# Two rows of turns of their own: for the first three groups, and for what is left once the last group has begun

## The chip, the cores and the metric

The kernel runs on one core of a Trainium2 chip. Its engines work side by side, each through its own queue: TensorE (PE, with its weight loads as PEld), VectorE (DVE), ScalarE (ACT), GpSimd (POOL) and SyncE (SP), which here only issues transfers. The metric is the device time of one execution in microseconds (us), the median over runs.

## What is computed

Four graph layers are applied one after the other to 64 graphs of 256 nodes with 256 features; each layer gets the features x and the graph's adjacency matrix, and its result is added to x and normalised:

```python
x = layernorm(x + L0(x, adj))   # q, k, v projections, 4 heads, masked softmax, Wo, layernorm
x = layernorm(x + L1(x, adj))   # layernorm, 8 heads with q = k = v, masked softmax,
                                # layernorm, gelu(y @ W1 + b1) @ W2 + b2 (256 -> 1024 -> 256)
x = layernorm(x + L2(x, adj))   # Wh = x @ W; e = leaky_relu(s1[i] + s2[j]), masked softmax, e @ Wh
x = layernorm(x + L3(x, adj))   # e = leaky_relu((x * a0) @ x.T), softmax where adj == 1, e @ x
```

All is float32. The graphs don't depend on each other; within a graph the layers do.

## The kernel before

**Groups.** The 64 graphs are worked in 32 groups of two (`G = 2`). A graph of 256 nodes is two blocks of 128 rows, so a group's activations are tiles of 128 partitions x 4 blocks x 256 features. A group is a Python generator, `group(g)`: it records the instructions of a small step and yields. A call of `next` on it is a *turn*. Its steps in order:

- one turn to load x and adj of the group (SP, L439 and L441; for groups 0 and 1 the loads are already recorded ahead of the weights W1 and W2),
- one turn in which ACT turns adj into bfloat16 (`adjb`, L875, and a check, L876),
- one turn for the transposes of `adjb` by DMA (`adjT`, L883, four instructions on SP), then the mask on DVE (L886), which multiplies adjT by adjb,
- layer 0: transposes of x by PE (L519 `pm<-ident,x`) and their copy by ACT (`xT`, L572), projections with Wq and Wk (ACT writes `qT`, `kT`, L699) and Wv, then attention,
- layer 1: the same attention with q = k = v and eight heads, W1 with a gelu (`hT`, L774) and W2 (`project`, y at L687),
- layer 2 (`wx` projection, `ex`, the matrix `qT` at L829 and L831, the product `v,qT`) and layer 3 (`ps<-z,xT`, exponentials L857 and L858, DVE L859 and L861, the product `xn,qT`).

Every matmul is recorded at L516 and every PE transpose at L519, whatever the step, so the tiles tell them apart.

**Attention.** A chunk makes scores on PE (`ps`), ACT takes the exponential (`e`, L593), DVE multiplies by the mask: in layer 0 one instruction per tile (L595), in layer 1 one per 128 x 256 piece with a running sum (L601), 8 per chunk, 4 chunks per group. The products `e,v` or `e,z` of a chunk follow on PE after the scores of the next chunk. What comes after the products of a graph (`behind`) is spread over later turns. In layer 0 it is: the sums' reciprocals (`zs`, L629) go to DRAM (`lines`, L714) and come back spread over the partitions (`rr`, L716), DVE multiplies (`oT`, L718), PE multiplies with Wo (`pm<-L_gnn_WoT,oT`), DVE adds the bias (y, L725), then two normalisations (L532, L533 and L729 to L736 on DVE, L535 and L539 on POOL) lead to `z` and `xb`, which layer 1 starts from.

**Order.** PE's order is the order in which the turns are recorded: `in_order` ties each matmul to the one before. The order on the other engines is chosen when the program is built, by priorities that follow the recording and by what is ready in the builder's own reckoning; once built, each engine works through its queue from front to back. So the row of turns sets what stands behind what on every engine.

In steady state five to six groups of different ages are under way. One period of turns is `ORDER`, 45 digits; a digit is an age, and the group that gets the turn is `period - age`. Every group gets 45 turns in all: 1 in the period in which it begins, then 9, 13, 13, 6 and 3. The loop runs over 32 + 5 periods and leaves out groups that don't exist. In the first and the last periods the same row is thus played with holes: at the start a group's turns follow each other with few of other groups between them, and at the end likewise.

**Buffers.** x and adj have two buffers each (`io`), `adjb` and `adjT` one each, so a group's `adjb` waits for the mask of the group before it. Most activations have three (`AT_ONCE`), PSUM four tiles `pm` and two `ps`.

`prepare` is a further generator that makes constants (bias products, `bop`, `wx` columns, bounds); it goes forward one step with each turn of group 0 after the first five (`PREPARE`).

Of the kernel before, what the change touches and what calls it, by code (L numbers as in the profile page):

```python
# [32 lines left out]
END = "end"  # L33
AT_ONCE = 3


ORDER = "011225334342343542234235432323132121321132121"
PREPARE = 5


# [355 lines left out]
def usual_input(ctx: ExitStack, tc: tile.TileContext, a: dict, out: bass.AP, flag: bass.AP):  # L396
# [574 lines left out]

    groups = [group(g) for g in range(B // G)]
    preparing = prepare()
    own = 0
    for period in range(len(groups) + int(max(ORDER))):
        for age in ORDER:
            g = period - int(age)
            if 0 <= g < len(groups):
                next(groups[g], END)
            if g == 0:  # L980
                own += 1
                if own > PREPARE:
                    next(preparing, END)
    assert all(next(g, END) == END for g in groups)


# [18 lines left out]
@with_exitstack  # L1005
def four_layers(ctx: ExitStack, tc: tile.TileContext, a: dict, out: bass.AP):
    nc = tc.nc
    keep = ctx.enter_context(tc.tile_pool(name="keep", bufs=1))
    flag = keep.tile([1, 1], I32, name="flag")
    usual_input(tc, a, out, flag)  # L1010
    unusual = nc.values_load(flag)
    with tc.If(unusual > 0):
        any_input(tc, a, out)
# [25 lines left out]
```

## Time and profile before

| | before |
|---|---|
| device time, median of 3 | 2674.66 us (2673.68 to 2675.3) |
| span of the profiled execution | 2673.3 us, granted TensorE clock 0.989 |
| PE busy | 2589.8 us (97%) |
| DVE busy | 1968.5 us (74%) |
| ACT busy | 1291.3 us (48%) |
| POOL busy | 587.3 us (22%) |
| the chain that ended last | PE 70%, DVE 17%, POOL 9% |

A row of the profile names the engine, the line, the operation, the tile it writes and the tiles it reads, and how many instructions it stands for; in brackets is the idle time of the engine just before it and what ended it. Idle time of an engine that others don't wait for costs nothing. The granted clock is the share of its full speed at which TensorE was let run. What is read from these views, stretch by stretch, is in the prediction.

### The profile page before, as it was taken

How to read it: one execution, taken by the hardware profiler on the slowest of the kernel's cores; microseconds unless marked ns; L12 is line 12 of the kernel's file. 1: busy time of each engine (PE TensorE's matmuls, PEld its weight loads, DVE VectorE, ACT ScalarE, POOL GpSimd, SP SyncE). 2: the span in 40 equal slices, each digit the busy share in tenths (PEclk: the TensorE clock that was granted, in tenths of full speed). 3: DMA queues.
4: the chain of work that ended last, by engine and by line, in shares of the span. 5: the costliest groups of instructions: out<-in, count | busy, mean ns of one | idle time of the engine just before them, and what ended most of it. 6: DMA issues, size and time to landing. Idle time of an engine off the chain costs nothing.

```text
span 2673.3 us, 44868 instructions
## 1 busy us (share of the span) xinstructions
PE 2589.8 (97%) x16648; PEld 1764.3 (66%) x16648; DVE 1968.5 (74%) x6189; ACT 1291.3 (48%) x1995; POOL 587.3 (22%) x1139
## 2 busy tenths in 40 slices
PE   5899999999999999999999999999999999999996
PEld 2466676676676676676676676676676676676665
DVE  4657777777777777777777777777777777777764
ACT  3445444555444555444455444455445455445442
POOL 1212222222222222222222222222222222222221
PEclk8899999999999999999999999999999999999998
DMA  5000110010110010110010110010110010000000
GB/s 154 25 9 22 35 37 25 29 36 21 36 36 25 29 37 21 36 37 25 29 36 21 36 36 25 29 35 22 36 36 25 29 32 25 29 29 17 17 9 17
DMA packets 113728, 83.20 MB, mean 31 GB/s; under 512 B 44256, under 2 KB 113120, under 8 KB 113504
## 3 DMA queue, kind: packets, MB, share of 16 engines
q1 hardware_dynamic: 112416, 79.74, 9.9%
q8 instruction: 134, 2.20, 0.3%
q14 instruction: 90, 0.74, 0.1%
q10 hardware_dynamic: 1088, 0.53, 0.1%
HBM read 54.80 MB, written 17.04 MB: 27 GB/s over the span
## 4 chain that ended last, share of the span: by engine, by line
PE 70%; DVE 17%; POOL 9%; issue 2%; DMA 1%; SPq 1%; ACT 0%; DVEq 0%; POOLq 0%; ACTq 0%
PE pm L516 54%; PE ps L516 10%; PE pm L519 7%; POOL rstd L539 6%; DVE st L532 3%; DVE y L802 2%; DVE y L730 2%; DVE xn L547 2%; POOL ve L535 2%; DVE z L547 2%; DVE mv L533 1%; DVE y L729 1%; DVE xb L736 1%; DVE e L601 1%; DVE r L801 1%
## 5 line engine op out<-in xcount | busy, mean ns | idle before, releaser
L601 DVE SCALAR_TENSOR_TENSOR e<-e,mask 128x256 f32<-128x256 f32 x1024 | 430.3, 486 | 131.6 <-ACT e L593 131.6
L593 ACT ACTIVATE e<-ps 128x1024 f32<-128x1024 f32 x384 | 371.9, 1019 | 195.1 <-PE ps L516 178.4
L516 PE MATMUL pm<-L_gnn_W,hT 128*128 128x256 f32 x2048 | 462.7, 379 | 0.0
L516 PE MATMUL pm<-xT,L_gnn_W 128*128 128x512 f32 x1024 | 456.2, 594 | 0.0
L516 PEld LDWEIGHTS pm<-L_gnn_W,hT 128*128 128x128 f32 x2048 | 384.6, 190 | 48.8 <-issue 0.3
L774 ACT ACTIVATE hT<-pm,b 128x512 f32<-128x512 f32 x256 | 176.9, 691 | 417.7 <-PE pm L516 417.6
L516 PEld LDWEIGHTS pm<-xT,L_gnn_W 128*128 128x128 f32 x1024 | 192.6, 191 | 204.5 <-issue 199.7
L532 DVE BATCH_NORM_STATS2 st<-y 128x6 f32<-128x256 f32 x768 | 301.4, 408 | 6.7
L539 POOL TENSOR_TENSOR rstd<-ve,mhalf 128x2 f32<-128x2 f32 (+1 forms) x384 | 298.1, 776 | 26.6
L547 DVE TENSOR_SCALAR xn<-y,mv,rstd 128x256 f32<-128x256 f32 x384 | 141.6, 410 | 180.1 <-POOL rstd L539 180.1
L535 POOL TENSOR_SCALAR ve<-mv 128x2 f32<-128x2 f32 x384 | 98.5, 257 | 757.7 <-DVE mv L533 757.2
L760 POOL TENSOR_TENSOR both<-y,xb 128x512 f32<-128x512 f32 x64 | 81.3, 1271 | 761.7 <-DVE y L759 761.7
L595 DVE TENSOR_TENSOR e<-e,mask 128x1024 f32<-128x1024 f32 x128 | 150.9, 1221 | 17.1 <-ACT e L593 17.1
L574 ACT ACTIVATE xT<-pm,beta,gamma 128x512 f32<-128x512 f32 x128 | 92.4, 770 | 126.1 <-PE pm L519 125.9
L516 PE MATMUL ps<-xT 32*128 32x256 f32 x2048 | 148.5, 402 | 0.3 <-ACT e L593 0.2
L516 PE MATMUL pm<-e,z 128*32 128x256 f32 x2048 | 141.3, 385 | 1.7 <-DVE e L601 1.4
L516 PEld LDWEIGHTS ps<-xT 32*128 32x128 f32 x2048 | 93.4, 185 | 72.8 <-issue 68.3
L516 PE MATMUL pm<-L_gnn_WoT,oT 128*128 128x256 f32 x512 | 120.4, 389 | 14.7 <-DVE oT L718 12.5
L516 PE MATMUL pm<-e,v 128*32 128x256 f32 x2048 | 125.2, 384 | 6.0 <-DVE e L595 6.0
L516 PE MATMUL ps<-qT,kT 64*128 64x256 f32 x1024 | 127.9, 389 | 0.3 <-ACT e L593 0.3
L516 PE MATMUL pm<-xT,L_gnn_WqT 128*128 128x512 f32 x256 | 121.5, 618 | 3.4 <-ACT xT L572 3.4
L516 PE MATMUL pm<-v,qT 128*128 128x260 f32 x512 | 119.5, 387 | 4.7 <-DVE qT L831 4.7
(136 smaller groups left out, 4058.7 us busy)
## 6 DMA issues: line engine op xcount, KB each, us to landing
x<-in_x SPq DMA_DIRECT2D x32, 512.0 KB
adj<-in_adj SPq DMA_DIRECT2D x32, 512.0 KB
rr<-lines SPq DMA_DIRECT2D x128, 128.0 KB
out<-xn SPq DMA_DIRECT2D x31, 512.0 KB
L_gnn_W<-in_L_gnn_W SPq DMA_DIRECT2D x2, 1024.0 KB
adjT<-adjb SPq DMA_TRANSPOSE x128
lines<-zs SPq DMA_DIRECT2D x64, 4.0 KB
out<-xn SPq DMA_DIRECT2D x2, 256.0 KB
```

The source lines that it names most:

```text
L516: in_order(nc.tensor.matmul(*args, **kw))
L519: in_order(nc.tensor.transpose(*args))
L532: nc.vector.bn_stats(st[:, q, :], src[:, t, 0:D])
L535: nc.gpsimd.tensor_scalar(ve[:, 0], mv[:, :, 1], EPS, None, ALU.add)
L539: nc.gpsimd.tensor_tensor(rstd, ve, mhalf[:, 0:k * QB].rearrange("p (k t) -> p k t", k=k), ALU.pow)
L547: nc.vector.tensor_scalar(dst[:, t, 0:D], src[:, t, 0:D], mv[:, q, 0:1], rstd[:, q:q + 1], ALU.subtract, ALU.mult)
L574: nc.scalar.activation(dst[:, c, on], pt[:, on], AF.Identity, bias=bias[:, c:c + 1], scale=scale[:, c:c + 1])
L593: nc.scalar.activation(e, ps, AF.Exp, scale=scale)
L595: nc.vector.tensor_tensor(e, e, mask.unsqueeze(1).to_broadcast([P, 2, QB * N]), ALU.mult)
L601: nc.vector.scalar_tensor_tensor(e[:, h, k], e[:, h, k], 1.0, mask[:, k], ALU.mult, ALU.mult, accum_out=sums[:, kc, c, j:j + 1])
L760: nc.gpsimd.tensor_tensor(both[:, i * QB:(i + 1) * QB, 0:D], o, xi, ALU.add)
L774: nc.scalar.activation(hT[:, f, :], pm, AF.Gelu, bias=b1[:, f:f + 1])
```

## The change

The first three groups (with one turn of the fourth) get a row of 34 turns of their own, `FIRST`, in which a digit is the group's number. After it the periods go on as before, but a turn that a group has already had in advance is left out (`due` counts the turns that the periods ask for, `done` those that were given). Once the last group has begun, at the end of period 31, the 113 turns that are left are given by `LAST`, in which a digit counts back from the last group. The number of turns of each group stays 45, and what a turn does is unchanged. It is for the two ends of the program, in which the one row for all periods has holes: the turns can be placed there for what the few groups under way need.

```diff
+FIRST = "3100000000021101000001010000010111"
+LAST = ("001142322312324311231243212120210102100210100031121201213200120132101010010120100010101102"
+        "01021000001000010010000")
...
-    own = 0
-    for period in range(len(groups) + int(max(ORDER))):
+    done = [0] * len(groups)
+    due = [0] * len(groups)
+
+    def turn(g):
+        done[g] += 1
+        next(groups[g], END)
+        if g == 0 and done[0] > PREPARE:
+            next(preparing, END)
+
+    for g in FIRST:
+        turn(int(g))
+    for period in range(len(groups)):
         for age in ORDER:
             g = period - int(age)
-            if 0 <= g < len(groups):
-                next(groups[g], END)
-            if g == 0:
-                own += 1
-                if own > PREPARE:
-                    next(preparing, END)
+            if g >= 0:
+                due[g] += 1
+                if due[g] > done[g]:
+                    turn(g)
+    for back in LAST:
+        turn(len(groups) - 1 - int(back))
```

In the row as it was played before, the first turns went to the groups `0 1 0 0 0 0 0 0 0 0 0 2 1 1 0 0 0 0 0 0 0 0 1`; now they go to `3 1 0 0 0 0 0 0 0 0 0 2 1 1 0 1 0 0 0 0 0 1 0`. Group 3's load of x and adj is recorded first of all (it was the 35th turn), and three turns of group 1 (its x transposes, its Wq and its Wk projections) come some turns earlier among those of group 0. After 35 turns both rows have given the same turns, and they are the same until shortly before the end: from turn 1334 on (`LAST` begins with turn 1328) they differ at 14 places, by exchanges of turns that are near each other.

## The prediction

> **What bounds the kernel now.** I read the busy time by stretch first, then TensorE in order of time at both ends, then the engines it waits for.
>
> Start, end and everything between (columns: stretch, length, busy us of PE, PEld, DVE, ACT, POOL, then granted clock, DMA share, GB/s):
>
> ```profile
> 0.00:130.00 130.00, 83.76 (x537) 49.18 (x538) 70.82 (x194) 47.43 (x72) 19.54 (x40) 0.84 0.32 88
> 130.00:2550.00 2420.00, 2408.24 (x15620) 1645.17 (x15619) 1827.41 (x5750) 1207.64 (x1858) 548.06 (x1050) 1.00 0.10 29
> 2550.00:2674.00 124.00, 97.81 (x493) 69.94 (x492) 70.31 (x245) 36.21 (x65) 19.67 (x51) 0.93 0.04 14
> ```
>
> In the 2420 us between, PE idles 11.8 us at full clock: nothing to win. It idles 130 - 83.8 = 46.2 us at the start and 26.2 us at the end, at clocks of 0.84 and 0.93. The change touches just these.
>
> PE at the start (start us, length, what; in brackets the idle time before it and its cause):
>
> ```profile
> 34.01 1.07 PE L516 MATMUL pm<-e,v 128*32 128x256 f32 x16
> 40.40 1.93 PE L516 MATMUL pm<-e,v 128*32 128x256 f32 x16 [5.31 <-DVE e L595]
> 54.89 5.44 PE L516 MATMUL pm<-L_gnn_WoT,oT 128*128 128x256 f32 x16 [10.85 <-DVE oT L718]
> 69.36 0.78 PE L519 MATMUL pm<-ident,z 128*128 128x128 f32 x2 [9.03 <-DVE rstd L542]
> 73.26 1.72 PE L519 MATMUL pm<-ident,z 128*128 128x128 f32 x6 [3.12 <-DVE z L547]
> 77.02 1.97 PE L519 MATMUL pm<-ident,x 128*128 128x128 f32 x8
> 83.87 3.70 PE L516 MATMUL pm<-xT,L_gnn_WqT 128*128 128x512 f32 x8
> 89.58 3.70 PE L516 MATMUL pm<-xT,L_gnn_WkT 128*128 128x512 f32 x8
> ```
>
> Group 0 has holes of 28 us in its layer 0, while group 1's transposes and q/k projections, ready from x alone, come at 77 to 93. VectorE (DVE) and the DMA queue (SP) make two of the holes:
>
> ```profile
> 37.97 1.23 DVE L886 SCALAR_TENSOR_TENSOR mask<-adjT,adjb 128x1024 bf16<-128x1024 bf16 x1 [4.51 <-DMA adjT<-adjb]
> 39.12 1.22 DVE L595 TENSOR_TENSOR e<-e,mask 128x1024 f32<-128x1024 f32 x1
> 46.14 1.24 SPq L714 DMA_DIRECT2D lines<-zs  x2
> 49.84 2.67 SPq L716 DMA_DIRECT2D rr<-lines  x4
> 52.60 5.07 SPq L883 DMA_TRANSPOSE adjT<-adjb  x4
> ```
>
> Group 0's last e stands behind group 1's mask; its reciprocal sums leave after three groups' transposes. At the end (PE, then DVE):
>
> ```profile
> 2567.99 2.97 PE L516 MATMUL pm<-e,z 128*32 128x256 f32 x16
> 2582.57 3.74 PE L516 MATMUL pm<-wx,xT 128*128 128x259 f32 x16 [1.03 <-DVE r L801]
> 2594.32 5.43 PE L516 MATMUL pm<-v,qT 128*128 128x260 f32 x16 [2.88 <-DVE qT L831]
> ```
> ```profile
> 2590.82 1.90 DVE L829 TENSOR_SCALAR qT<-pm,ex 128x256 f32<-128x256 f32 x4
> ```
>
> The last group's layer 1 is paced by DVE there: the e,z product takes 2.97 us where the one at 2485.41 took 1.07.
>
> **What the Trainium skill says.**
> - "TensorE: Matmul & The Clock Gate", What's actually happening: after an idle window of some 3.4 us the array runs at half clock. The trace agrees: WoT took 5.44 us after the 10.85 us hole and 3.62 us at 2522.39. A filled hole pays twice.
> - Same page, Architectural detail: DVE and ScalarE (ACT) queues are strictly first in, first out. The trace agrees (e behind the mask above).
> - [...]Here the 4 KB of lines took 3.7 us from issue to the issue of rr.
> - "GPSIMD Engine Reference", Specifications: its SBUF interfaces are shared with VectorE. The trace agrees: beside GpSimd's x+beta (79.07, 2.44 us) one e product (79.22) took 2.57 us instead of 0.42.
>
> **The change, part by part.** The built program's order shows what moved. No work is added. PE's stream differs in two places: around the first 88 of some 3270 rows, and in some 80 rows near the end; the middle is identical, so what the start wins stays won.
>
> Start, step by step:
> 1. Group 0's last e stands ahead of group 1's mask on DVE: it follows the e before it (cast done near 33.4), so it ends near 34.6 instead of 40.3; PE ends these products at 37 instead of 44. Against it, group 3's adj (512 KB) is now loaded ahead of group 0's transposes: at the 332 to 405 GB/s of that stretch 1.4 us on the first mask (0 if the transposes hide it, 2 at 250 GB/s). Taken: 38.4.
> 2. The first graph's lines leave after two groups' transposes, near 39; + 3.7 + 4.2 (rr at 49.84 to its product at 54.05) = 47, so its WoT half runs inside the hole. The second graph's rr stands behind group 2's transposes (5.05) and adj issue (0.58): issue near 50, + 4.2 = 54, product 0.7, WoT half at slow clock 3.6 (54.89 to the first y at 58.64): its y at 58.3 instead of 60.64. The first graph's y stands behind that product on DVE, so this second one sets the chain: -2.3. Group 1's x transposes and Wq, Wk (1.0 to 2.0 + 7.4 us of PE) lie in the holes around.
> 3. From y to z the chain is DVE and GpSimd, unchanged. PE is warm when z comes: transposes 0.8 instead of 1.72, scores 1.15 instead of 2.09. Layer 1's first masked e: 78.18 - 2.3 - 1.8 = 74.1.
> 4. Group 0's layer 1 loses its filler and becomes DVE-paced: 32 products at 0.346 us (1.04 for three in the run after 90.09) = 11.1, + 0.25, + 1 for refills; 12.4 instead of 98.22 - 78.18 = 20.0. The near row is the end stretch, where 24 took 2567.36 to 2575.90 without a break. GpSimd's x+beta has gone elsewhere. Sum -11.7.
> 5. Group 1's scores used to run beside that and now follow the last e,z: they give back about 1. Its second WoT no longer waits (2.26, DVE mv): its oT product now stands ahead of the first y. -11.7 + 1 - 2.3 = -13.0; I keep 1.5 back, since step 4 allows one refill where four chunks could need one each, and take -11.5. Ends: -7 (about 2 us more at three chunks) to -14 (WoT also warm: 1.89 at 191.45 where 3.62 is counted).
>
> SBUF for x also changes hands: group 3's x takes group 0's buffer and group 2's takes group 1's. Group 2's x thus leaves at the place of the second load (128.79) instead of 67.02; PE wants it at 152.07. With some 4 us of transfer (3.8 for an adj load in the chain at 25.55) 19 us are over, and both ends shift together: nothing.
>
> End, step by step:
> 6. Half of the second W2 product (3.5 us) moves between the second and third score chunks of group 31, and group 30's 3.6 us xn,qT products ahead of the last e,z; on DVE the e products come before the two xn scalings. So e is ready sooner and the waits are filled: wx starts near 2578.4 instead of 2582.57, -4.2.
> 7. Next PE wants xb, which DVE delivers near 2584.7 instead of 2586.4: 2 us of new wait. But the ex transposes then meet a free DVE (group 29's statistics now come later, into the 10.54 us at 2604.8 in which DVE idles), so qT is done near 2589 instead of 2594.2 and the 2.88 wait with its slow product (5.43 instead of 3.67) goes. At that product: -6; if the new wait cools the clock, -4.
> 8. In the last 45 us xn,qT goes ahead of ex and xn transposes. It fills 0.70 + 0.55 us, but v,qT then waits for DVE's 0.99 + 0.69 after ex: it starts at 2636.4 in both. Nothing.
> Taken for the end: -5, ends -2 and -7.
>
> Sum: -11.5 - 5 = -16.5; 2674.66 - 16.5 = 2658.2.
>
> **The rivals.**
> - A, the round trip stays: the added adj loads (before the first transposes, and 0.6 us before the second rr) push the second rr by another 1.5 us, and layer 1 without filler stalls at each chunk. Start -2.3 + 1.5 = -0.8, -1.8 for the clock, layer 1 in 16.6 instead of 20, + 1 given back: -5; end -2: 2667.7. For it: the DMA rows run at up to 1.18 busy share until 27.5. Against: the trace's own 24 unbroken products.
> - B, the start as forecast, the end given back: xb's new wait with a cold clock eats steps 6 and 7: 2674.7 - 11.5 = 2663.2. For it: xb's last scaling moves by just 1.7 us. Against: two waits of DVE's queue disappear.
> - C, slower: group 2's x comes late, or the late masks hold up group 1's layer 0, and the start wins nothing; some 5 us lost, 2680. Against: the 19 us of slack.
>
> **How the numbers follow.** Forecast 0.72, A 0.14, B 0.09, C 0.05. The forecast's ends are -9 and -21, 2653.7 to 2665.7. With A in part and unknown clocks: 2652 to 2668. 0.2% is 5.3 us, so faster means below 2669.3: forecast, B and most of A, 0.90; same 0.06; slower 0.04.
>
> **What would show it.** In the new profile: PE's e,v products end near 38; WoT in two pieces with Wq and Wk behind them before 69; the run of L601 over group 0 some 12 us long instead of 20; W1's first product near 112 instead of 124.28; group 2's x not among the waits. At the end no wait on qT L831 of 2.9 us, a new one on xb. Wrong, if the first mask is late by more than 2 us, if layer 1's e products come in four separated runs, or if PE's idle time in the first 130 us stays above 40.

## The result, and the profile after

| | before | after |
|---|---|---|
| device time, median (range) of 6 runs each | 2672.90 us (2669.84 to 2675.30) | 2664.86 us (2660.80 to 2667.29) |
| ratio after / before | | 0.9969, 95% interval 0.9956 to 0.9981 |
| span of the profiled execution | 2673.3 us | 2659.4 us |
| granted TensorE clock in it | 0.989 | 0.992 |

The change saves 8 us (5 to 12 by the interval); 16.5 were forecast, and 2658.2 against 2664.86 us in the end. In a second set of runs, beside the experiments below, the same kernel took 2664.95 us against 2675.46 for before: 0.9959 (0.9945 to 0.9972), or 10.5 us. Neither interval holds 0, and neither holds 16.5 us. The profiled execution of after (2661.17 us) is one of the shortest of its six and that of before (2675.07 us) lies at the long end of its range, so the 13.9 us between the two spans overstate the gain.

In the profile after, every line number is 5 higher than before up to L970, and 15 higher beyond L985 (L601 is L606 now). The three stretches of after (columns as in the prediction: busy us of PE, PEld, DVE, ACT, POOL, granted clock, DMA share, GB/s):

```profile
0.00:130.00 130.00, 92.94 (x563) 54.70 (x564) 74.28 (x208) 51.97 (x78) 22.57 (x44) 0.88 0.33 92
130.00:2540.00 2410.00, 2398.03 (x15596) 1640.61 (x15595) 1823.01 (x5736) 1203.64 (x1852) 546.62 (x1044) 1.00 0.10 29
2540.00:2660.00 120.00, 93.92 (x493) 68.33 (x491) 70.79 (x245) 36.06 (x65) 19.80 (x52) 0.94 0.04 14
```

PE's idle time in the first 130 us went from 46.2 to 37.1 us; at the end it is 26.1, as it was (26.2), though in a stretch 4 us shorter. The middle idles 12 us in both. So the idle time that went, went from the start; the rest of the 13.9 us is 4.9 us less of busy time for the same matmuls. Of the 13.9 us, 10.1 lie ahead of group 31's bias product and 3.6 behind it. PE in the start:

```profile
47.08 3.75 PE L521 MATMUL pm<-L_gnn_WoT,oT 128*128 128x256 f32 x8 [7.69 <-DVE oT L723]
56.80 3.75 PE L521 MATMUL pm<-L_gnn_WoT,oT 128*128 128x256 f32 x8 [5.97 <-DVE oT L723]
68.91 0.63 PE L524 MATMUL pm<-ident,z 128*128 128x128 f32 x2 [0.87 <-DVE rstd L547]
72.81 1.72 PE L524 MATMUL pm<-ident,z 128*128 128x128 f32 x6 [3.27 <-DVE z L552]
108.79 0.47 PE L524 MATMUL pm<-ident,xb 128*128 128x128 f32 x1 [5.12 <-DVE xb L552]
110.84 4.62 PE L521 MATMUL pm<-L_gnn_WoT,oT 128*128 128x256 f32 x16
115.30 13.90 PE L521 MATMUL pm<-xT,L_gnn_W 128*128 128x512 f32 x32
```

WoT (the product with Wo) now runs in two halves, as expected, but PE is no warmer (no nearer to its full clock) than before when z comes: the six transposes take 1.72 us, to the hundredth what they took at 73.26. W1 starts at 115.30 instead of 124.28. DVE in the same stretch (the last row stands right behind layer 1's last masked e of group 0), then the same two ends of layer 1 before, then the DMA queue after:

```profile
34.92 1.22 DVE L600 TENSOR_TENSOR e<-e,mask 128x1024 f32<-128x1024 f32 x1
55.96 0.69 DVE L723 TENSOR_TENSOR oT<-oT,rr 128x512 f32<-128x512 f32 x1 [3.18 <-DMA rr<-lines]
60.59 0.69 DVE L730 TENSOR_TENSOR y<-pm,bop 128x512 f32<-128x512 f32 x1 [1.95 <-PE pm L521]
77.72 0.43 DVE L606 SCALAR_TENSOR_TENSOR e<-e,mask 128x256 f32<-128x256 f32 x1 [3.79 <-ACT e L598]
90.14 0.69 DVE L761 TENSOR_TENSOR y<-pm,r 128x512 f32<-128x512 f32 x1
```
```profile
78.18 0.42 DVE L601 SCALAR_TENSOR_TENSOR e<-e,mask 128x256 f32<-128x256 f32 x1 [3.79 <-ACT e L593]
98.22 0.69 DVE L756 TENSOR_TENSOR y<-pm,r 128x512 f32<-128x512 f32 x1
```
```profile
39.35 0.61 SPq L719 DMA_DIRECT2D lines<-zs  x1
45.22 5.07 SPq L888 DMA_TRANSPOSE adjT<-adjb  x4
51.04 1.25 SPq L721 DMA_DIRECT2D rr<-lines  x2
```

Group 0's last e ends at 36.1 instead of 40.3 and its first lines leave at 39.35. But the second broadcast (51.04) still follows group 2's four transposed loads. Its product on DVE ends at 56.65, and the second y stands at 60.59 against 60.64 before: four microseconds won early are gone here. The first masked e of layer 1 starts at 77.72 against 78.18. But the run of masked e takes 12.4 us where it took 20.0: this is most of what the start wins.

The end, on PE and then on DVE (group 31's bias product, from which I count, is at 2546.58 before and 2536.48 after):

```profile
2569.35 1.06 PE L524 MATMUL pm<-ident,xn 128*128 128x128 f32 x8 [1.64 <-DVE y L807]
2577.39 1.66 PE L524 MATMUL pm<-ident,xb 128*128 128x128 f32 x6 [2.10 <-DVE xb L552]
2583.62 3.67 PE L521 MATMUL pm<-v,qT 128*128 128x260 f32 x16
```
```profile
2566.42 2.19 DVE L552 TENSOR_SCALAR xn<-y,mv,rstd 128x256 f32<-128x256 f32 x4
2576.92 0.74 DVE L552 TENSOR_SCALAR xb<-y,mv,rstd 128x256 f32<-128x256 f32 x2 [1.14 <-POOL rstd L544]
```

The wait of 2.88 us for qT is gone and the v,qT product is warm (3.67, not 5.43). In exchange PE waits 2.10 us for xb.

### The profile page after: what moved, and what is told of

It reads as the page before. It is cut to its first block, busy times and chain, and to the rows that moved or that the text cites. A ratio compares the mean times of both kernels' runs of the same rounds, so it can differ in the third digit from the quotient of the medians.

```text
span 2659.4 us, 44866 instructions
## 1 busy us (share of the span) xinstructions
PE 2584.9 (97%) x16648; PEld 1763.6 (66%) x16648; DVE 1968.1 (74%) x6189; ACT 1291.7 (49%) x1995; POOL 589.0 (22%) x1139
## 4 chain that ended last, share of the span: by engine, by line
PE 71%; DVE 16%; POOL 8%; issue 2%; DMA 1%; SPq 1%; ACT 1%; DVEq 0%; ACTq 0%; POOLq 0%
PE pm L521 55%; PE ps L521 10%; PE pm L524 7%; POOL rstd L544 6%; DVE st L537 3%; DVE y L807 2%; DVE y L735 2%; DVE xn L552 2%; POOL ve L540 2%; DVE z L552 2%; DVE mv L538 1%; DVE y L734 1%; DVE xb L741 1%; DVE r L806 1%; SPq L888 1%
## 5 line engine op out<-in xcount | busy, mean ns | idle before, releaser
L606 DVE SCALAR_TENSOR_TENSOR e<-e,mask 128x256 f32<-128x256 f32 x1024 | 428.1, 482 | 128.9 <-ACT e L598 128.9
L544 POOL TENSOR_TENSOR rstd<-ve,mhalf 128x2 f32<-128x2 f32 (+1 forms) x384 | 298.2, 776 | 26.7
```

Of the source, the lines that this page charges most:

```text
L544: nc.gpsimd.tensor_tensor(rstd, ve, mhalf[:, 0:k * QB].rearrange("p (k t) -> p k t", k=k), ALU.pow)
L606: nc.vector.scalar_tensor_tensor(e[:, h, k], e[:, h, k], 1.0, mask[:, k], ALU.mult, ALU.mult, accum_out=sums[:, kc, c, j:j + 1])
```

## The experiments

**A common zero.** The first mask on DVE (28.07 us before, 29.62 after) shifts with the transfers of the first 30 us: between 29.62 and 31.73 in the traces that load group 3 first. So the start is measured from it to group 31's bias product, and the end from there to the last matmul of the program. This leaves out what the new first load costs the first mask itself: on two chips it comes 0.9 to 1.8 us later than with the old order of loads (`last_only`, `load3_late`). With that cost in, and on one chip, group 31's bias product stands at 2538.67 us in `first_only` and at 2547.91 in `last_only`: 9.2 us. All times are medians of 5 rounds and more; "before" was timed on the same chip.

| kernel | time, us | before, us | ratio (95%) | start | end |
|---|---|---|---|---|---|
| before | | | | 2518.51 | 120.45 |
| after | 2664.86 | 2672.90 | 0.9969 (0.9956 to 0.9981) | 2506.86 | 116.87 |
| after_again | 2664.95 | 2675.46 | 0.9959 (0.9945 to 0.9972) | 2507.46 | 118.59 |
| first_only | 2666.21 | 2674.54 | 0.9969 (0.9958 to 0.9981) | 2507.44 | 120.48 |
| last_only | 2672.43 | 2674.54 | 0.9993 (0.9985 to 1.0001) | 2517.96 | 117.31 |
| load3_late | 2664.16 | 2674.27 | 0.9960 (0.9947 to 0.9974) | 2509.24 | 116.88 |
| rr_first | 2660.73 | 2674.54 | 0.9953 (0.9939 to 0.9967) | 2504.39 | 116.95 |
| v_early | 2663.67 | 2674.54 | 0.9963 (0.9949 to 0.9977) | 2505.45 | 118.70 |
| rr_mask_v | 2658.25 | 2675.46 | 0.9936 (0.9923 to 0.9950) | 2500.73 | 118.12 |
| xb_early | 2662.69 | 2675.46 | 0.9951 (0.9937 to 0.9965) | 2504.65 | 118.51 |
| best | 2658.18 | 2675.46 | 0.9939 (0.9925 to 0.9952) | 2503.67 | 115.61 |
| w2_back | 2662.68 | 2674.27 | 0.9958 (0.9945 to 0.9972) | 2506.65 | 116.80 |
| best3 | 2659.60 | 2675.71 | 0.9938 (0.9924 to 0.9952) | 2504.65 | 116.61 |
| best2 | 2659.26 | 2675.71 | 0.9937 (0.9923 to 0.9951) | 2501.30 | 119.14 |

**1. Which row brings what?** `first_only` keeps the new first row and plays the end in the order of before; `last_only` keeps the end alone.

```diff
# first_only (digits 69 to 95 of LAST; two exchanges elsewhere too)
-LAST = "...101001012010001010110201021..."
+LAST = "...101100101002001010102101021..."
# last_only
-FIRST = "3100000000021101000001010000010111"
+FIRST = ""
```

> The start as changed, the end in the order of before. Theory (two gains that add up, -10 us at the start and -3.6 at the end): W1's first product at 115 to 116, the bias product of group 31's layer 2 near 2536.5, the last matmul near 2657 instead of 2653.35; the time 2 to 4 us above the changed kernel. Rival (the start is everything, the end's new order wins nothing once clocks are alike): the same time as the changed kernel within 1.5 us.

> The end as changed, the start as before. Theory (gains that add up): W1's first product at 124.3 as before, from group 31's bias product to the last matmul 116.9 us as in the changed kernel instead of 120.5; the time 2 to 4 us below before, near 2669. Rival (the end wins nothing): the time of before within 1.5 us.

The start alone gives 8.3 us (0.9969), the end alone 2.1, with an interval that reaches just over 1. In the traces they are independent: W1 starts at 117.30 with the new row (31.23 its first mask) and at 126.41 without (29.95), and the end takes 120.48 in the old order and 117.31 in the new. So the two parts add up. The end's own length depends on the run: 120.45 and 120.48 us in the two traces of the old order, 115.6 to 119.1 us in the traces of the new one (the table's last column), so 1.3 to 4.9 us less. This spread is one reason why the profiled pair differs by more than the medians. The rival "the start is everything" is not excluded by the times alone.

**2. Is the profiled run typical?** The changed kernel once more, unaltered.

> The changed kernel, nothing altered, timed beside the experiments. Theory (its runs differ by where TensorE's slow-clock stretches fall, and the profiled run shown was one of its fast ones): the ratio to before stays at 0.996 to 0.998, and in this trace the stretch from group 31's bias product to the last matmul, 116.87 us in the run shown and 118.70 with one digit moved at the start, falls anywhere between 116.9 and 119. Rival (the 13.9 us between the two profiled runs are the effect): ratio 0.995, 116.9 again.

Ratio 0.9959, end 118.59: the theory holds. The row of instructions is that of after, yet the WoT product behind the 5.12 us wait takes 5.17 us (4.62 in the run shown, 3.62 when warm), and what follows W1's second block in the end takes 67.69 us instead of 66.22. The Trainium skill ("TensorE: Matmul & The Clock Gate", What's actually happening) says that the window by which the clock is judged runs free, so that the number of slow matmuls at a kernel's start differs from run to run. This trace pair shows such a difference behind a hole in mid-kernel too, and its 0.6 to 1.5 us are as large as some effects sought here.

**3. Did the earlier sums of steps 1 and 2 bring anything?** Moving one digit puts the DMA queue and DVE back in the order of before, with PE's order kept.

```diff
-FIRST = "3100000000021101000001010000010111"
+FIRST = "1000000000211010000010100000101113"
```

> The changed kernel with group 3's first turn (its adjacency load) moved from the first to the last place of the row. TensorE's order stays that of the changed kernel, but the DMA queue and VectorE go back to the order of before: group 0's last e behind group 1's mask, both lines and broadcasts behind group 2's transposed loads. Theory (steps 1 and 2 won nothing, since the second y stands at 60.59 against 60.64 before; all of the start's gain is TensorE's order): the first mask comes 1.3 to 1.5 us earlier, the second y near 60, W1's first product near 115 (counted from the first e,v product 83 to 86 us instead of 83.05), the time within 2 us of the changed kernel. Rival (the earlier sums of the first graph are part of the gain): second y later than 62, TensorE colder before z, the time 3 us or more above the changed kernel.

DVE of this kernel (first mask, group 0's last e, second y):

```profile
29.88 1.23 DVE L891 SCALAR_TENSOR_TENSOR mask<-adjT,adjb 128x1024 bf16<-128x1024 bf16 x1 [7.42 <-DMA adjT<-adjb]
40.92 1.22 DVE L600 TENSOR_TENSOR e<-e,mask 128x1024 f32<-128x1024 f32 x1
62.41 0.69 DVE L730 TENSOR_TENSOR y<-pm,bop 128x512 f32<-128x512 f32 x1
```

The last e is 4.4 us late again (36.52 in w2_back, which ran beside it), but the first mask is 1.34 us sooner (31.22 there), and the second y 1.08 us later (61.33 there). W1 then starts 1.32 us later (117.79 against 116.47) and the time is 1.5 us more, within both intervals. So steps 1 and 2 together are worth some 1.3 us and not 2.3; this experiment's "nothing" was slightly off too, and the second y (62.41) came past the rival's 62. The 1.3 us rest on one pair of traces: counted from the first mask, W1 starts after 85.25 to 86.70 us in four traces of after's own order, so chance alone could make them. The other 9 us of the start (2518.51 to 2509.24) came with the new order of turns on TensorE, which this kernel keeps.

**4. What held the second round trip?** `rr_first` ties group 2's transposed loads to group 0's second broadcast, by an order alone.

```diff
+                came = nc.sync.dma_start(rr[...], lines[...])
+            if g == 0:
+                back_again.append(came.ins.name)
...
+            ins = nc.sync.dma_start_transpose(pt[...], adjb[:, t, :])
+            if g == 2:
+                tc.add_manual_dep(ins.ins, back_again[-1], ...)
```

> The changed kernel, but group 2's transposed adjacency loads are told to leave after group 0's second broadcast of reciprocals. Theory (step 2 failed because the second broadcast stands behind these four transposed loads and one plain load on the DMA queue): the second broadcast is issued near 47.7 instead of 51.04, its product is done near 52 instead of 56.65, the second y stands near 55.5 instead of 60.59, and all up to W1 is 4 to 5 us earlier (W1 near 111); the time 3 to 5 us less. Rival (the chain is held by VectorE's queue or by the length of the round trip, not by its place in the queue): the second y stays within 1.5 us of 60.6, or group 2's later mask takes back what is won, and the time is within 1.5 us of the changed kernel.

DVE between the second round trip and the second y (lines are 3 to 7 higher in this kernel):

```profile
53.85 0.69 DVE L726 TENSOR_TENSOR oT<-oT,rr 128x512 f32<-128x512 f32 x1 [4.70 <-DMA rr<-lines]
56.71 1.22 DVE L898 SCALAR_TENSOR_TENSOR mask<-adjT,adjb 128x1024 bf16<-128x1024 bf16 x1 [1.56 <-DMA adjT<-adjb]
57.86 0.42 DVE L538 BATCH_NORM_STATS2 st<-y 128x6 f32<-128x256 f32 x1
58.22 0.69 DVE L733 TENSOR_TENSOR y<-pm,bop 128x512 f32<-128x512 f32 x1
```

From the first mask, the second oT is done 23.1 us later instead of 27.0 in after, and the second y comes 26.7 instead of 31.0 us later (30.1 and 30.2 in w2_back and v_early, whose order is that of after there): 3.4 to 4.2 us sooner, so the place in the DMA queue was the cause of these. Only 2.5 of it reach the end of the start (2504.39 against 2506.86; 3.1 against `first_only` on the same chip). W1 came at 114.67 where 111 was expected, and the interval of the time (0.9939 to 0.9967) overlaps that of after_again. The rival was right in its second half: group 2's later mask takes a part back. The lines show why: group 2's mask now stands ahead of the first graph's statistics (57.86, ready since 55.1), DVE waits 1.56 us for it and then works 1.2 us on it, and both graphs' normalisations follow in one lump.

**5. Was PE cold at z because of its holes?** `v_early` has group 1's Wv projection in them.

```diff
-FIRST = "3100000000021101000001010000010111"
+FIRST = "3100000000021101000001011000000111"
```

> The changed kernel with group 1's Wv projection ahead of group 0's z transposes on TensorE (one digit of the row moved). Theory (step 3 failed because TensorE still idles 0.87 + 3.27 us before these transposes and is at half clock when they come): the six z transposes take about 0.8 us instead of 1.72 and the 16 score products about 1.15 instead of 2.09, the first masked e comes near 75.8 instead of 77.72, W1 near 113.4; the time 1 to 2 us less. Rival (the clock is not set by this hole): transposes and scores stay at 1.72 and 2.09, or Wv delays the first two z transposes and these what follows, and the first masked e is no earlier; the time within 1 us.

PE of this kernel:

```profile
69.34 3.62 PE L521 MATMUL pm<-L_gnn_WvT,xT 128*128 128x256 f32 x16
74.13 1.16 PE L524 MATMUL pm<-ident,z 128*128 128x128 f32 x6 [0.95 <-DVE z L552]
75.72 1.15 PE L521 MATMUL ps<-xT 32*128 32x256 f32 x16 [0.43 <-ACT xT L579]
```

The filler leaves 0.95 us of wait, the transposes take 1.16 us (0.8 was expected) and the scores 1.15 instead of 2.09. The missing 0.9 us is the clock: the share granted at the scores is 0.50 in after and 1.00 here. The prediction's rule speaks of an idle window of some 3.4 us; in after, waits of 0.87 and 3.27 us with 0.63 us of work between them were enough for half clock, and these the prediction had overlooked. At xb (108.28, first mask 31.73) 2.0 to 2.6 us are won against w2_back and after, 1.0 to 1.9 of them up to the first masked e; why the rest came was not looked into. WoT's slow stretch behind the wait for xb takes up to 1.1 of it back (5.68 us against 4.62). In the time nothing is to be seen: 0.9963 lies between the two ratios of after.

The filler is no guarantee either. `rr_mask_v` (experiment 6) has it too, and there the wait for z is 1.86 us; the six transposes take 1.16 us, but the scores right behind them are at a granted clock of 0.50 again:

```profile
68.83 2.09 PE L523 MATMUL ps<-xT 32*128 32x256 f32 x16 [0.43 <-ACT xT L581]
```

In `best2` the same scores take 1.15 us behind a wait of 1.71 us.

**6. Both, with group 2's mask out of the way.** `rr_mask_v` adds to 4 and 5 that group 2's mask on DVE comes after group 0's layer 0.

```diff
+FIRST = "3100000000021101000001011000000111"
...
+        if g == 2:   # ins: the mask's instruction; layer0_done: names of group 0's xb scalings
+            tc.add_manual_dep(ins.ins, layer0_done[-1], ...)
```

> The changed kernel with three edits: group 2's transposed loads behind group 0's second broadcast, group 2's mask behind group 0's layer 0 on VectorE, group 1's Wv projection ahead of the z transposes on TensorE. Theory (in the kernel with the first edit alone the second y came 4.2 us earlier, and 1.9 us of it was lost because group 2's mask stood ahead of the first graph's statistics; with the third edit alone 2.6 us came from the clock): counted from the first e,v product, W1's first product at 83.05 - 4.2 - 2.3 = 76.5 us, or 79 if Wv then stands in the way of the z transposes; the time 4 to 6 us below the changed kernel. Rival (the two gains are the same gain): 80.5 us, no better than the first edit alone.

W1 starts at 110.94, 77.1 us after the first e,v product at 33.81 (76.5 expected), and the time is 6.7 us below after_again on the same chip, where no run of the one lies in the range of the other. So the gains add up to what was expected, although the scores, which 0.9 us of it were to come from, are slow in this trace.

**7. The new wait for xb in the start.** `xb_early` gives group 0 two turns more ahead of group 1's last three, and four behind them.

```diff
-FIRST = "3100000000021101000001010000010111"
+FIRST = "3100000000021101000001010000010001110000"
```

> The changed kernel with six more turns of group 0 in the first row: its second half of layer 1 and its scalings xb ahead of group 1's e products on VectorE, and half of its W1 products ahead of group 1's WoT on TensorE. Theory (the new 5.12 us wait for xb comes from group 1's four e products and two reciprocals, 4.67 + 2 x 1.76 us, standing ahead of group 0's y on VectorE): the wait falls below 2 us, W1's first product comes near 106 instead of 115.30, and the bias product behind all W1 and WoT products near 125 instead of 129.03; the time 2 to 4 us below the changed kernel. Rival (group 1's e,v products, its sums and its round trip then come later by what is won): bias product at 128 to 130, time unchanged.

PE of this kernel (e,v products of group 1, group 1's z transposes):

```profile
101.91 2.21 PE L521 MATMUL pm<-e,v 128*32 128x256 f32 x32 [1.73 <-DVE e L600]
132.53 1.16 PE L524 MATMUL pm<-ident,z 128*128 128x128 f32 x6 [2.16 <-DVE z L552]
```

The wait of 5.12 us is gone, so it did come from the e products and reciprocals ahead of y on DVE. W1 and WoT are through 94.9 us after the first mask instead of 99.4. But a wait of 1.73 us for e and one of 2.16 for z take its place; about 2.2 to 2.8 of the 4.5 us last to the end of the start, and 2.3 us in the time.

**8. All together, and two attempts to keep more.** `best` joins 6 and 7; `best3` has a quarter of W1 ahead of WoT instead of half; `best2` also mixes y and xb among group 1's e products.

```diff
+FIRST = "3100000000021101000001011000000001110000"   # best
+FIRST = "310000000002110100000101100000000111000"    # best3
+FIRST = "310000000002110100000101100000010110000"    # best2
# and, in all three, the two orders of experiments 4 and 6
```

> All of these edits together (transposed loads of group 2 later, its mask later, Wv earlier, xb and half of W1 earlier). Theory (they work on different holes, so the gains add): the bias product that ends the start, 129.03 in the changed kernel with the first e,v product at 32.25 (96.8 us between them), comes 87 to 90 us after the first e,v product; the time 7 to 10 us below the changed kernel. Rival (one chain on VectorE holds all of it): 92 us or more, no better than the best of the single edits.

> The kernel with all edits together, with a quarter of W1 ahead of group 1's WoT instead of half. Theory (in the kernel with all edits the z transposes of group 1 waited 2.16 us because WoT, and so all of group 1's chain to z, came 7 us of W1 later; this gave back what the early xb had won): the wait for z goes, both halves of W2 take 3.62 us, and the time is 2 to 3 us below the version with three edits, near 0.9928 of before. Rival (WoT then waits for the broadcast itself): WoT waits 1 to 3 us, the time that of the version with three edits, 0.9936 to 0.9939.

> As the one before it, but with the second half of group 0's y and xb placed between group 1's e products on VectorE instead of ahead of them. Theory (the e,v products of group 1 waited 2.29 + 1.71 us for e in the kernel with all edits, since y and xb stood ahead of e): these waits fall below 1 us in all, and the time is 1 us below the one before it. Rival (the sum of VectorE's work up to the reciprocals is the same in any order, so the broadcast and WoT come no sooner): within 1 us of the one before it.

All three stand at 0.9937 to 0.9939, where rr_mask_v already was (0.9936): what 7 gave alone is not added to it. In best the bias product came 89.7 us after the first e,v product, as expected, but behind it z waits 2.16 us and the next W2 half takes 5.04 us instead of 3.62. In best3 the wait for z is gone and WoT's second half waits 2.25 us instead, for statistics on DVE (mv). In best2 the e,v waits are still 0.57 to 1.11 us each. Every version of this stretch moves the hole to another place, which points to one chain on DVE up to group 1's z; it was not isolated. The rivals of `best3` and `best2` were right.

**9. Why the end gave less.** `w2_back` undoes the first half of step 6.

```diff
-LAST = "...001012010..."
+LAST = "...100012010..."
```

> The changed kernel with the half of group 31's second W2 product that was put between its second and third score products put back ahead of the second ones; xn,qT stays ahead of the last e,z. Theory (step 6 fell short because y on VectorE now waits 1.46 us for that half and its sums stand between the second and the third chunk of e, so that e ends only 1.1 us sooner): counted from group 31's bias product, the last e ends near 27 us instead of 28.2, wx starts 33 us after it instead of 34.23, xb waits less, and the second block of W1 starts 49.5 us after it instead of 50.65. Rival (VectorE has the same work before xb either way): e ends sooner but wx and W1 do not; W1 at 50.5 to 51.5. Times within 2 us of the changed kernel in both.

DVE of this kernel (y of the W2 half that was moved back; the row behind the last e):

```profile
2555.18 0.69 DVE L692 TENSOR_TENSOR y<-pm,both 128x512 f32<-128x512 f32 x1 [3.32 <-PE pm L521]
2565.86 0.68 DVE L761 TENSOR_TENSOR y<-pm,r 128x512 f32<-128x512 f32 x1
```

Counted from the bias product at 2537.87, e ends at 27.99 (28.18 in after), wx starts at 34.05 (34.23) and W1's second block at 50.54 (50.65). The rival was right: DVE waits 3.32 us for this half instead of 1.46, and then runs on without a break. The place of the W2 half doesn't matter (0.1 us), and my theory on step 6 falls.

## Why the prediction was right, and where it fell short

The range (2652 to 2668 us) held, the forecast's own figure did not: 8 us were saved in one set of runs and 10.5 in the other, where 16.5 were written. The measured 2664.86 us lies 6.7 us above the forecast's 2658.2 and nearer to rival B's 2663.2 and rival A's 2667.7; that the range reached far enough is owed to rival A having been let into it. The time alone doesn't tell the three apart. The traces do, step by step:

1. Last e ahead of the mask: right. It ends at 36.1, PE's products with it at 38.4 as taken, and the first mask is 1.55 us later (1.4 taken; 1.34 in experiment 3).
2. The second y at 58.3: wrong. It stood at 60.59, 0.05 us sooner than before in that pair, 1.1 on one chip (experiment 3) and 1.8 on another (62.94 in last_only, 61.12 in first_only). The working put 4.2 us from the issue to the start of the product (4.9 measured, 51.04 to 55.96) and had the issue at 50, where it came at 51.04. Experiment 4 shows what the round trip was worth once it isn't behind the transposed loads. Missing: 0.5 to 2.2 us.
3. PE warm at z: wrong. It would have been warm had the holes been filled, but Wq and Wk end at 68.0 and z comes in two parts, with 0.87 and 3.27 us of waiting. Experiment 5 gives the 0.9 us of the scores back in one trace. And 0.4 us of the term were never there: six z transposes behind a short wait take 1.16 us at full clock (2550.91 in before) and not 0.8. Missing: 1.8 us; the first masked e came at 77.72 instead of the 74.1 forecast.
4. Layer 1 paced by DVE, 12.4 us: right. It runs from 77.72 to 90.14 with two gaps of 0.44 us. This -7.6 us carries the result.
5. From its end to W1: 25.2 us instead of 26.1, -0.9 where -1.3 was taken. The 2.26 us wait of WoT is gone, but xb's wait grew from 3.82 to 5.12 us. With the 1.5 us kept back, the start came to -9.0 instead of -11.5 at W1, and to -10.1 at group 31's bias product, as W1's own block took 13.90 instead of 15.11. Group 2's x was not waited for.
6. wx 4.2 us sooner: wrong in size. It starts 34.23 us after the bias product instead of 35.99: -1.8. The last e ends only 1.1 us sooner, and then the xn transposes wait 1.64 us for y L807, which stands behind four xn scalings on DVE (2.19 us beside a sum of GpSimd at 2566.18; two alone take 0.73).
7. xb and v,qT: the signs were right, the size not. xb was to be ready 1.7 us sooner and is ready 1.3 us later, counted so. The traces name the link that I missed: with xn,qT and the xn transposes ahead of them, the last oT transposes of group 31 start 33.8 us after the bias product instead of 30.1, and y and xb follow from them. PE cools there (the granted clock is 0.50 behind the 2.10 us): xb (six of its eight transposes), ex and W1 take 1.66, 1.06 and 4.10 us instead of 1.16 (all eight), 0.60 and 3.70. W1's second block is 2.4 us sooner where 6, or 4 with a cold clock, was written. Moving oT alone was not tried, so this link is read from the order of the rows and not shown by a run.
8. The tail swap: right. From W1's second block to the first late v,qT 36.70 us, 36.83 before. Behind that the profiled pair differs by 1.1 us more, but not through the order: the last two xn,qT products took 2.73 and 3.33 us in before and 1.91 and 1.96 in after, but 3.42 and 2.57 in after_again.

So the side and the order of the parts were right, and the size was not: 2 to 4 us are missing at steps 2 and 3 and 2 to 3 at steps 6 and 7, of which the reserve of 1.5 us made up a part. This accounts for the 13.9 us of the profiled pair; from there to the 8 and 10.5 us of the medians no step is to be named, only the spread of the runs. Rival A's doubt (the added load ahead of the second broadcast) was the right one on step 2, and wrong on layer 1, where it had stalls at each chunk. Rival B's doubt came true in kind: xb's new wait with a cold clock ate about half of the end's 5 us, and not all.

## What to carry to other kernels

Fill the holes of an engine by recording other work there, but look at what is queued behind the late step on *every* queue: here four transposed loads ahead of a small broadcast held the next step up by 3 to 4 us, and with these moved, a mask ahead of statistics took 1 to 2 back. Counting only the first hole closed is not enough to call an engine warm; check each wait left ahead of the work that is to be fast. And where each new order only moves the hole, as in experiment 8, one engine's queue may hold the whole chain: look for it before trying a further order.

## What the hardware showed that I had not expected

- The six runs of after lie near 2661, 2664.9 and 2667.3 us, two at each, with mean clocks of 0.992 to 0.988. The same 16 WoT matmuls behind the same wait of 5.12 us took 4.62, 4.79, 5.14 and 5.17 us in four traces with the same order at that place.
- Four transposed loads hold the DMA queue for 5.07 us, 1.27 us each (at 45.22 in after; those at 19.38 hold it for 7.2 us), and a broadcast of a few KB waits behind them.
- Waits shorter than the prediction's 3.4 us can bring half clock: 0.87 and 3.27 us with a little work between them did in after, 1.86 us did in `rr_mask_v`, and 1.71 us in `best2` did not.
- One load of 512 KB issued before the first transposes delays the first mask by 0.9 to 1.8 us on two chips (1.34 in the pair of experiment 3); between traces with nothing changed ahead of it that mask moved by up to 2.1 us.
